# Routing the first rows of a mixture of experts: four gate quadrants at once, running maxima, weight columns in threes

## The chip, the core and the metric

The kernel runs on one core of a Trainium2 chip. The core has TensorE (PE, with its weight loads as PEld), VectorE (DVE), ScalarE (ACT), GpSimd (POOL) and SyncE (SP), each with a queue of its own that it works off in order; DMAs are issued from SP, ACT and POOL. The metric is the device time of one execution in microseconds, the median of several runs.

## The reference

`x` has 64 x 64 tokens of 256 channels, `cond` one row of 64 for each batch entry. There are 8 experts of three layers (256 to 512 to 512 to 256), two of them for each token, all in float32.

```python
var = jnp.mean(x * x, axis=-1, keepdims=True)
xn = rms_w * (x * jax.lax.rsqrt(var + EPS))
gate = xn @ wg_W + wg_b + (genre_embed @ gg_W + gg_b)
gate_w = jax.nn.softmax(gate, axis=-1)
topk_w, topk_i = jax.lax.top_k(gate_w, TOP_K)
cw = jnp.sum(jax.nn.one_hot(topk_i, E, dtype=x.dtype) * topk_w[..., None], axis=-2)
h1 = jax.nn.relu(jnp.einsum('bsh,ehm->bsem', x, W1) + b1)
h2 = jax.nn.relu(jnp.einsum('bsem,emn->bsen', h1, W2) + b2)
out_e = jnp.einsum('bsen,enh->bseh', h2, W3) + b3
return x + jnp.einsum('bseh,bse->bsh', out_e, cw)
```

## The kernel before

Only the two chosen experts of a token are computed. Tokens are sorted by expert into tiles of 128 rows; a tile runs through the three layers of one expert, and its result, scaled by the token's weight for that expert, is added to the output rows by an indirect DMA. The output first receives a copy of `x` (the "fills", DMAs from DRAM to DRAM).

The order of instructions is written out by hand (`manual_schedule`), so each engine's queue stands as the code calls it. The stages are:

- *First part* (`first_part`). Token `p * 32 + i` lies in partition `p`, column `i`. The first 8 columns are part A (1024 tokens), the other 24 part B. Rows are loaded in 8 groups of 4 columns (`load_x` on SP), squared and summed (`squares`, L184 on DVE, L182 on ACT), turned by PE (`turn`, L193; the copies out of PSUM are L204 on DVE and L206 on ACT) and multiplied by the gate weights (`gates`, L211): a matmul writes 32 of the 128 PSUM partitions, a quadrant, and the two halves of the channels are summed there one after the other. `upright` turns the gates back. `Part.root` and `Part.norm` give the inverse root of the mean square; `Part.choose` finds the two highest gates on DVE and writes one-hot rows `oh`; `count` makes running counts `inc` by expert (L312), `totals` sums them over partitions on PE (L324, L325). From part A's counts come slots, a one-hot table `hotA` (L459), and by 16 small matmuls `idxA` (L469), the tokens of the first tile of each expert. `gather` (L680, POOL) then fetches the rows of tile 0 (`xg`), and the weights of the later experts may load.
- *Head steps* `u` = 0 to 6 (`head_step`): layer 1 (L797, relu on ACT L800), turning of the next tile's rows (L733), layer 3 of the tile before (L824), layer 2 (L808, relu L811). In between, `rest` is handed out in pieces (`more`): it routes part B and builds the table of all later tiles (L613, L615, L620 on DVE, L520 on PE), up to `idxR` (L634). `pA.weights` and `pA.spread` (L347 to L350) write the token weights to `cwdA` in DRAM; `gather_cw` fetches the weight columns `cg` of a tile. `scaled` makes `bc` (bias times weight, L784 on ACT), and `give` makes `y` (L833, DVE) and adds it to the output (L834, POOL). The adds wait for each other, and the first one for the fill.
- *Later steps* (from tile 8, the first whose expert is only known at run time): tiles are taken in pairs where they can be, weights are copied on DVE to a fixed place (L758, L763, L767), and rows are turned through DRAM (`stow`, `shuffle`) and DVE (L722). A switch on the number of tiles ends the kernel.

The weights of all experts (`w1a`, `w2a`, `w3a`) are loaded on SP: the three of expert 0 right behind the rows and the biases `vecs` (the source of `vT`, L500), the others after the gather of tile 0. PE's PSUM banks 0, 1, 2 and 5 serve the turned rows, then banks 0 to 3 the layers. POOL makes the identity matrix and clears buffers (L941, L943, L381) before its first DMAs.

Of the kernel before, what the change touches and what calls it, by code (L numbers as in the profile page):

```python
# [21 lines left out]
def kernel(  # L22
# [86 lines left out]
    make_identity(nc, ident)  # L109
    ones = const.tile([P, P], F32, name="ones")  # L110
    nc.gpsimd.memset(ones, 1.0)
# [4 lines left out]
    nc.gpsimd.dma_start(gg_sb[G : G + 1, :], gg_b.unsqueeze(0))  # L116
    nc.gpsimd.dma_start(gg_sb[G + 1 : G + 2, :], wg_b.unsqueeze(0))
    seg = const.tile([P, E, NB], F32, name="seg")
    nc.gpsimd.memset(seg, 1.0)
    nc.gpsimd.memset(seg[:, :, 0:1], 0.0)  # L120
    segA = const.tile([P, E, NA], F32, name="segA")
    nc.gpsimd.memset(segA, 1.0)
    nc.gpsimd.memset(segA[:, :, 0:1], 0.0)
    segT = const.tile([P, NB, E], F32, name="segT")
    nc.gpsimd.memset(segT, 1.0)
    nc.gpsimd.memset(segT[:, :, 0:1], 0.0)
# [81 lines left out]
    def gates(c, bufs, bank=PB[3], q0=0):  # L208

        for q, n in enumerate(bufs, q0):  # L210
            nc.tensor.matmul(  # L211
                bank[32 * q : 32 * q + 32, :],
                lhsT=wg_sb[:, c, :],
                rhs=turned(n),
                start=(c == 0),
                stop=(c == HC - 1),
            )

    def upright(nq, bank=PB[3], dst=PB[4], copied=False):

        R = 32 * nq
        if not copied:
            nc.scalar.copy(gTs[0:R, :], bank[0:R, :])
        gtp = dst[:, 0 : TPB * R].rearrange("p (k r) -> p k r", k=TPB)
        for k in range(TPB):
            nc.tensor.transpose(gtp[:, k], gTs[0:R, ts(k, P)], ident[0:R, 0:R])
        return gtp.rearrange("p k (q e) -> p q k e", q=nq)[:, :, :, 0:E]

    def busy(n):

        for _ in range(n):
            nc.tensor.transpose(PB[6][:, 256 : 256 + P], ident, ident)

    class Part:


        def __init__(self, z, i0, i1):
            self.i0, self.i1, self.n, self.z = i0, i1, i1 - i0, z
            n = self.n
            self.t = {a: t2(f"{a}{z}", n) for a in ("var", "root", "y", "t", "rstd", "m1", "m2", "den", "d2")}  # L240
            self.gate, self.w = t3(f"gate{z}", n), t3(f"w{z}", n)
            self.oh, self.pr = (buf(gx, [P, TOPK, n, E], f"{a}{z}") for a in ("oh", "pr"))
            self.inc = buf(gx, [P, E, n], f"inc{z}")
            self.seg = segA if z == "A" else seg
# [113 lines left out]
    def load_weights(e):  # L358
        w = nc.sync.dma_start(w1a[:, e], W1[e].rearrange("(p c) m -> p c m", c=HC))
        if e:  # L360
            loads.append(w)
# [667 lines left out]
```

## Time and profile before

| | us |
|---|---|
| median of 3 runs | 519.79 (519.06 to 520.1) |
| profiled execution | 521.81 |
| its span | 520.0 |
| PE busy | 499.9 |
| DVE busy | 231.9 |
| ACT busy | 167.9 |
| POOL busy | 291.0 |
| first layer 1 (L797) starts | 25.18 |
| layer 1 of tile 8 starts | 98.59 |

The span runs from the first to the last instruction of the profiled execution; 1.8 us of its time lie around it. A row of a timeline has start, length, engine, line, operation, what is written and read, the sizes and how many instructions; in brackets the idle time before it and what ended that. A float32 matmul has two records. The mean granted TensorE clock was 0.984 of full speed.

### The profile page before, as it was taken

To read this page: it belongs to the slowest core of one execution; us is meant where nothing else is said; L and a number is where in the kernel's file an instruction comes from. 1 tells how busy PE (TensorE), PEld (TensorE's weight loads), DVE (VectorE), ACT (ScalarE), POOL (GpSimd) and SP (SyncE) were. 2 spreads that over 40 slices of the span, in tenths; PEclk is the share of its full clock that TensorE was granted. 3 is DMA by queue.
4 is the path that set the end of the run, shared out by engine and by line. 5 is a ranking of instruction groups with operands and counts; after the bars stand their busy time and mean duration, and the time that the engine had idled before them with its cause. 6 is when DMAs were issued, how large, how long until landed. Compare 5 with 4: busy or idle time off the path is not lost. (4 is left out here: it accounts for less than half of the span.)

```text
span 520.0 us, 8641 instructions
## 1 busy us (share of the span) xinstructions
PE 499.9 (96%) x2834; PEld 447.8 (86%) x2834; DVE 231.9 (45%) x560; ACT 167.9 (32%) x405; POOL 291.0 (56%) x243
## 2 busy tenths in 40 slices
PE   8899979999999999999999999999999999999992
PEld 6579969988888888888888888888888889999991
DVE  5768934343334333344444433433333336555550
ACT  5654324422222222222222222222222223443340
POOL 6314438776655566556566666566566455764521
PEclk9899979999999999999999999999999999999997
DMA  8799993343334343334343333333333333433201
GB/s 333 240 387 404 390 374 109 51 110 77 74 65 89 67 83 69 75 79 83 78 83 74 74 80 75 80 70 80 75 76 75 54 71 53 96 64 74 42 5 22
DMA packets 68160, 59.26 MB, mean 114 GB/s; under 512 B 39663, under 2 KB 59330, under 8 KB 67588
## 3 DMA queue, kind: packets, MB, share of 16 engines
q1 hardware_dynamic: 52464, 41.21, 24.1%
q0 software_dynamic: 15200, 17.32, 20.8%
q8 instruction: 25, 0.41, 0.3%
q14 instruction: 35, 0.29, 0.2%
q10 hardware_dynamic: 436, 0.03, 0.1%
HBM read 42.80 MB, written 20.71 MB: 122 GB/s over the span
## 5 line engine op out<-in xcount | busy, mean ns | idle before, releaser
L808 PE MATMUL pb<-hid,big 128*128 128x256 f32 (+1 forms) x1120 | 210.8, 346 | 0.0
L808 PEld LDWEIGHTS pb<-hid,big 128*128 128x128 f32 x1120 | 187.0, 191 | 20.4
L834 POOL DMA_INDIRECT out_dram<-y,idxR x59 | 97.2, 1648 | 131.3 <-issue 61.4
L811 ACT ACTIVATE hid<-pb,bb 128x256 f32<-128x256 f32 (+1 forms) x140 | 61.5, 440 | 245.7 <-PE pb L808 240.4
L763 DVE COPY big<-w2a 128x2048 f32 x35 | 44.2, 1262 | 162.6 <-PE pb L808 156.8
L797 PE MATMUL pb<-xT,big 128*128 128x256 f32 (+1 forms) x560 | 108.2, 346 | 0.0
L824 PE MATMUL pb<-big,hid 128*128 128x256 f32 x472 | 107.6, 379 | 0.0
L797 PEld LDWEIGHTS pb<-xT,big 128*128 128x128 f32 x560 | 93.5, 191 | 9.9
L824 PEld LDWEIGHTS pb<-big,hid 128*128 128x128 f32 x472 | 88.8, 190 | 11.5
L680 POOL DMA_INDIRECT big<-in_x_dram,idxR x59 | 80.0, 1355 | 20.7 <-issue 16.5
L680 POOL DMA_INDIRECT cg<-cwdR,idxR x59 | 70.1, 1189 | 18.1 <-issue 18.1
L800 ACT ACTIVATE hid<-pb,bb 128x256 f32<-128x256 f32 (+1 forms) x140 | 61.5, 440 | 40.9 <-PE pb L797 26.8
L833 DVE SCALAR_TENSOR_TENSOR y<-pb,cw,bc 128x256 f32<-128x256 f32 x59 | 28.5, 484 | 47.6 <-issue 25.6
L758 DVE COPY big<-w1a 128x1024 f32 x35 | 24.3, 695 | 25.8 <-PE pb L797 22.6
L808 PE MATMUL pb<-hid,w2a 128*128 128x128 f32 x256 | 30.3, 276 | 0.8 <-ACT hid L800 0.8
L808 PEld LDWEIGHTS pb<-hid,w2a 128*128 128x128 f32 x256 | 29.7, 192 | 1.2 <-ACT hid L800 1.0
L767 DVE COPY big<-w3a 128x1024 f32 x35 | 25.5, 729 | 0.5 <-issue 0.5
L834 POOL DMA_INDIRECT out_dram<-y,idxA x8 | 13.5, 1684 | 19.0 <-DVE big L620 6.7
L782 DVE TENSOR_SCALAR bc<-b_sb,cw 128x256 f32 x59 | 22.8, 386 | 2.2 <-DVE cw L779 0.2
L797 PE MATMUL pb<-xT,w1a 128*128 128x128 f32 x128 | 18.0, 297 | 4.8 <-ACT hid L811 3.9
L722 DVE STREAM_TRANSPOSE xT<-gTs 128x256 f32<-128x256 f32 x57 | 22.4, 423 | 0.0
L797 PEld LDWEIGHTS pb<-xT,w1a 128*128 128x128 f32 x128 | 16.7, 209 | 5.3 <-ACT hid L811 4.2
(212 smaller groups left out, 249.2 us busy)
## 6 DMA issues: line engine op xcount, KB each, us to landing
w2a<-in_L_cond_W_dram SPq DMA_DIRECT2D x8, 1024.0 KB
scr<-big SPq DMA_DIRECT2D x57, 128.0 KB
gTs<-scr SPq DMA_DIRECT2D x228, 32.0 KB
w1a<-in_L_cond_W_dram SPq DMA_DIRECT2D x8, 512.0 KB
w3a<-in_L_cond_W_dram SPq DMA_DIRECT2D x8, 512.0 KB
out_dram<-in_x_dram SPq DMA_DIRECT2D x4, 768.0 KB
big<-in_x_dram SPq DMA_DIRECT2D x4, 512.0 KB
big<-in_x_dram SPq DMA_DIRECT2D x2, 1024.0 KB
```

Of the source, the lines that this page charges most:

```text
L680: return nc.gpsimd.indirect_dma_start(out=dst, out_offset=None, in_=src, in_offset=bass.IndirectOffsetOnAxis(ap=index(b), axis=0), bounds_ ...
L758: V.tensor_copy(st1, w1a[:, e].rearrange("p e c m -> p (e c) m"))
L763: V.tensor_copy(st2, w2a[:, ex[u]].rearrange("p e c m -> p (e c) m"))
L767: V.tensor_copy(st3, w3a[:, ex[u]].rearrange("p e c m -> p (e c) m"))
L782: V.tensor_scalar(bc, b3e, cw, None, ALU.mult)
L797: nc.tensor.matmul(ph, lhsT=w1[:, c, ts(m, P)], rhs=cols[:, c, :], start=(c == 0), stop=(c == HC - 1))
L800: nc.scalar.activation(hids[:, 0, m, 0 : w * BT], ph, AF.Relu, bias=bb[:, 0, m : m + 1])
L808: nc.tensor.matmul(ph, lhsT=w2[:, m, ts(n, P)], rhs=hids[:, 0, m, 0 : w * BT], start=(m == 0), stop=(m == MC - 1))
L811: nc.scalar.activation(hids[:, 1, n, 0 : w * BT], ph, AF.Relu, bias=bb[:, 1, n : n + 1])
L824: nc.tensor.matmul(po, lhsT=hids[:, 1, n, ts(k, BT)], rhs=w3[:, n, :], start=(n == 0), stop=(n == MC - 1))
L833: V.scalar_tensor_tensor(y, sums(b), cw, bc, ALU.mult, ALU.add)
L834: add = nc.gpsimd.indirect_dma_start(out=orows, out_offset=bass.IndirectOffsetOnAxis(ap=index(b), axis=0), in_=y, in_offset=None, bounds_c ...
```

## The change

Part A's and the last gates use four quadrants at once, one for each group of rows and half of the channels (`gates_2`); the halves are added when the gates are turned back, by a matmul with `both`, two identity blocks one above the other (`upright_2`). The choice takes a running maximum along each token's 8 gates (a scan that starts anew at each token) in place of a maximum, an equality and a count of equals; one-hot rows are differences of neighbours, and are stored by expert, then column. The count is one scan over both choices; `totals` has three matmuls, one with a negative triangle. Part A takes its square root on ACT as before, part B by integer shift and three Newton steps on DVE. The table of part A is made in four pieces instead of two. All squares of part B and four copies of turned rows are on DVE. Part A's exponentials and `spread` come before the gathers of tiles 1 and 2. Weight columns are gathered three a step in steps 0, 1 and 2 (the last time two), into eight fixed places; `scaled` and `give` start in step 1. Of expert 0 only W1 is loaded ahead of the first gather, `b3` is loaded in two pieces, and most clears move from POOL to DVE, the load of `cond` from ACT to POOL. Longer removed pieces, which stand in the kernel above, are left out here.

```diff
+    nc.gpsimd.dma_start(cond_sb, cond)
+    nc.gpsimd.dma_start(gg_sb[G : G + 1, :], gg_b.unsqueeze(0))
+    nc.gpsimd.dma_start(gg_sb[G + 1 : G + 2, :], wg_b.unsqueeze(0))
     ones = const.tile([P, P], F32, name="ones")
-    nc.gpsimd.memset(ones, 1.0)
+    V.memset(ones, 1.0)
...
+    ntri = const.tile([P, P], F32, name="ntri")
+    V.memset(ntri, -1.0)
+    nc.gpsimd.affine_select(
+        out=ntri, in_=ntri, pattern=[[1, P]], compare_op=ALU.is_ge, fill=0.0, base=0, channel_multiplier=-1
+    )
+    both = const.tile([P, P // 2], F32, name="both")
+    nc.gpsimd.tensor_tensor(both, ident[:, 0 : P // 2], ident[:, P // 2 : P], ALU.add)
+    fresh = const.tile([P, NB, E], F32, name="fresh")
+    V.memset(fresh, 0.0)
+    V.memset(fresh[:, :, 0:1], -BIG)
...
-    def gates(c, bufs, bank=PB[3], q0=0):
-        for q, n in enumerate(bufs, q0):
+    def gates(c, bufs):
+        for q, n in enumerate(bufs):
             nc.tensor.matmul(
-                bank[32 * q : 32 * q + 32, :],
+                PB[3][32 * q : 32 * q + 32, :],
                 lhsT=wg_sb[:, c, :],
                 rhs=turned(n),
-                start=(c == 0),
-                stop=(c == HC - 1),
+                start=c == 0,
+                stop=c == HC - 1,
             )
...
+    def gates_2(bufs, bank):
+        for q, ns in enumerate(bufs):
+            for c, n in enumerate(ns):
+                r = 32 * (2 * c + q)
+                nc.tensor.matmul(bank[r : r + 32, :], lhsT=wg_sb[:, c, :], rhs=turned(n), start=True, stop=True)
+    def upright_2(dst):
+        gtp = dst[:, 0 : TPB * P // 2].rearrange("p (k r) -> p k r", k=TPB)
         for k in range(TPB):
-            nc.tensor.transpose(gtp[:, k], gTs[0:R, ts(k, P)], ident[0:R, 0:R])
-        return gtp.rearrange("p k (q e) -> p q k e", q=nq)[:, :, :, 0:E]
+            nc.tensor.matmul(gtp[:, k], lhsT=gTs[:, ts(k, P)], rhs=both, start=True, stop=True)
+        return gtp.rearrange("p k (q e) -> p q k e", q=2)[:, :, :, 0:E]
...
+            self.oh, self.pr = (buf(gx, [P, TOPK, n * E], f"{a}{z}") for a in ("oh", "pr"))
+            self.ohe = self.oh.rearrange("p k (e i) -> p k e i", e=E)
+            self.pre = self.pr.rearrange("p k (e i) -> p k e i", e=E)
+            self.slot = self.gate.rearrange("p i e -> p (i e)").rearrange("p (e i) -> p e i", e=E)
+            self.inc = buf(gx, [P, 1 + E * n], f"inc{z}")
+            V.memset(self.inc[:, 0:1], 0.0)
             self.cw8 = cw8B[:, i0:i1, :] if z == "B" else t3("cw8A", n)
+            same = gTs[:, 0 : n * (E + 1)] if z == "B" else t2("same", n * (E + 1))
+            self.same = same.rearrange("p (i e) -> p i e", i=n)
+            if z == "A":
+                V.memset(same, 0.0)
...
+        def along(self, t):
+            return t.unsqueeze(2).to_broadcast([P, E, self.n])
+        def norm(self, root):
+            var, y, t = (self.t[a] for a in ("var", "y", "t"))
+            V.tensor_scalar(var, ss[:, self.i0 : self.i1], 1.0 / H, EPS, ALU.mult, ALU.add)
+            if root:
+                nc.scalar.sqrt(t, var)
+                V.reciprocal(y, t)
+            else:
+                V.tensor_scalar(t.bitcast(I32), var.bitcast(I32), 1, None, ALU.arith_shift_right)
+                V.tensor_scalar(y.bitcast(I32), t.bitcast(I32), -1.0, float(0x5F3759DF), ALU.mult, ALU.add)
+            n = 1 if root else 3
+            for k in range(n):
+                V.scalar_tensor_tensor(t, y, -0.5, var, ALU.mult, ALU.mult)
+                V.tensor_tensor(t, t, y, ALU.mult)
+                V.scalar_tensor_tensor(self.t["rstd"] if k == n - 1 else y, t, 1.5, y, ALU.add, ALU.mult)
...
+            gf = gate.rearrange("p i e -> p (i e)")
+            tops = (self.pr[:, 1], self.cw8.rearrange("p i e -> p (i e)"))
+            ms = []
+            for k, (g, top) in enumerate(zip((gf, left), tops)):
+                V.tensor_tensor_scan(
+                    top, fresh[:, 0 : self.n].rearrange("p i e -> p (i e)"), g, 0.0, ALU.add, ALU.max
+                )
+                top = top.rearrange("p (i e) -> p i e", e=E)
+                m = top[:, :, E - 1]
+                ms.append(m)
                 yield
                 if k == 0:
-                    nc.gpsimd.tensor_tensor(self.w, gate, self.over_e(m1), ALU.subtract)
-                V.tensor_tensor(sc, g, self.over_e(m), ALU.is_equal)
+                    nc.gpsimd.tensor_tensor(self.w, gate, self.over_e(m), ALU.subtract)
+                V.tensor_tensor(self.same[:, :, 1:], top, self.over_e(m), ALU.is_equal)
                 yield
...
+                oh = self.ohe[:, k].rearrange("p e i -> p i e")
+                V.tensor_tensor(oh, self.same[:, :, 1:], self.same[:, :, 0:E], ALU.subtract)
                 yield
                 if k == 0:
-                    V.scalar_tensor_tensor(left, sc, -BIG, gate, ALU.mult, ALU.add)
+                    V.scalar_tensor_tensor(
+                        left.rearrange("p (i e) -> p i e", e=E), oh, -BIG, gate, ALU.mult, ALU.add
+                    )
                     yield
...
+            V.tensor_tensor_scan(self.inc[:, 1:], self.oh[:, 0], self.oh[:, 1], 0.0, ALU.add, ALU.add)
+            V.tensor_tensor(self.t["d2"], ms[1], ms[0], ALU.subtract)
...
+            at = self.inc[:, 0 : 1 + E * self.n : self.n]
+            nc.tensor.matmul(self.adj, lhsT=tri, rhs=at[:, 1:], start=True, stop=False)
+            nc.tensor.matmul(self.adj, lhsT=ntri, rhs=at[:, 0:E], start=False, stop=True)
+            nc.tensor.matmul(self.tot, lhsT=ones, rhs=at, start=True, stop=True)
+        def pick(self, dst):
+            V.tensor_tensor(self.pre, self.slot.unsqueeze(1).to_broadcast([P, TOPK, E, self.n]), self.ohe, ALU.mult)
             with nc.allow_low_precision(reason="one term of the sum is not 0, and ranks are exact"):
-                V.tensor_reduce(dst, self.pr, AX.X, ALU.add)
+                V.tensor_reduce(dst, self.pre.rearrange("p k e i -> p k i e"), AX.X, ALU.add)
...
+    def load_weights(e, parts=(0, 1, 2)):
+        for k in parts:
+            dst, src = (
+                (w1a[:, e], W1[e].rearrange("(p c) m -> p c m", c=HC)),
+                (w2a[:, e], W2[e].rearrange("(c p) n -> p c n", p=P)),
+                (w3a[:, e], W3[e].rearrange("(c p) h -> p c h", p=P)),
+            )[k]
+            loads.append(nc.sync.dma_start(dst, src))
+    left = [NA + i for i in (0, 1, 4, 5, 2, 3, 6, 7)] + list(range(NA + 8, NI))
+    def some(n):
+        for _ in range(n):
+            squares(left.pop(0), "V")
...
-        nc.gpsimd.memset(cw8B, 0.0)
+        V.memset(cw8B, 0.0)
+        for k in range(3):
+            V.memset(ring(run, [P, H], "xg", 3, k), 0.0)
+        V.memset(cgR, 0.0)
         nc.gpsimd.dma_start(cwdA.rearrange("(p i) e -> p i e", p=P)[:, NA:NI, :], cw8B[:, NA:NI, :])
-        busy(13)
-        for i, eng in enumerate("VVAA"):
-            squares(i, eng)
+        busy(12)
...
+        squares(TPB + 3, "A")
+        nc.tensor.transpose(cps, cond_sb, ident[:B, :B])
+        V.tensor_copy(condT[0:G], cps.unsqueeze(2).to_broadcast([G, B, REP]))
+        for i in (0, 1):
+            squares(TPB + i, "V")
         for j in range(NG - GA, NG):
             load_x(j)
         nc.sync.dma_start(vecs[0 : E * MC, :], b1.rearrange("e (c p) -> (e c) p", p=P))
         nc.sync.dma_start(vecs[E * MC : 2 * E * MC, :], b2.rearrange("e (c p) -> (e c) p", p=P))
...
+        load_weights(0, (0,))
+        gates_2(((0, 1), (2, 3)), PB[3])
+        pA.norm(True)
+        nc.scalar.copy(gTs, PB[3])
+        turn(GA, 0, 0, "A")
         nc.tensor.matmul(gps, lhsT=condT.rearrange("g b r -> g (b r)"), rhs=gg_sb, start=True, stop=True)
         V.tensor_copy(ggate, gps)
...
+        chosen = pA.choose(upright_2(PB[4]))
+        for q in (1, 2, 3):
...
+        pA.exps()
+        turn_pe(GA + 1, 1, 1)
+        gates(0, range(4))
         for q in range(2):
...
-        GH = GC // 2
+        GH = GC // 4
...
+        load_weights(0, (1, 2))
         tc.add_manual_dep(
-            loads[0].ins,
+            loads[1].ins,
             fetches[0].ins.name,
             mybir.DependencyInfo(mybir.DependencyClass.Sync, mybir.DependencyReason.DATA),
             reason="the first tile's rows go first",
         )
+        load_weights(1, (0,))
+        nc.sync.dma_start(b3_sb[:, 0:2], b3[0:2].unsqueeze(0).to_broadcast([P, 2, H]))
+        load_weights(1, (1, 2))
+        fills.append(nc.sync.dma_start(our[:, 0:NA, :], xr[:, 0:NA, :]))
         load_weights(2)
-        fills.append(nc.sync.dma_start(our[:, 0:NA, :], xr[:, 0:NA, :]))
-        nc.sync.dma_start(b3_sb, b3.unsqueeze(0).to_broadcast([P, E, H]))
+        nc.sync.dma_start(b3_sb[:, 2:E], b3[2:E].unsqueeze(0).to_broadcast([P, E - 2, H]))
...
+    def second_part():
         j0 = GA + 4
+        vps = PB[6][:, 384 : 384 + 2 * E * MC]
+        pA.weights()
+        some(1)
+        nc.tensor.transpose(vps, vecs, ident[: 2 * E * MC, : 2 * E * MC])
+        V.tensor_copy(vT.rearrange("p l e c -> p (l e c)"), vps)
+        some(1)
+        turn(j0, 0, 4, "V")
+        some(2)
+        turn(j0 + 1, 0, 6, "V")
+        gates(1, range(4))
+        some(2)
+        transpose_x(0)
         nc.scalar.copy(gTs, PB[3])
...
+        turn(j0, 1, 5, "V")
+        some(4)
+    def third_part():
+        turn(GA + 5, 1, 7, "V")
+        some(len(left))
+        raw = upright()
         nc.scalar.copy(graw[:, NA : NA + 4 * TPB, :].rearrange("p (q k) e -> p q k e", q=4), raw)
...
+        gates_2(((4, 5), (6, 7)), PB[7])
+        nc.scalar.copy(gTs, PB[7])
+    def last_upright():
+        nc.scalar.copy(
+            graw[:, NA + 4 * TPB : NI, :].rearrange("p (q k) e -> p q k e", q=2), upright_2(PB[6])
...
-        pA.exps()
         V.tensor_scalar(tokv, tokc, 0.0, None, ALU.is_ge)
         V.tensor_tensor(tokv, tokv, tokc, ALU.add)
         V.tensor_copy(tok16, tokv)
-        pB.norm()
...
+        V.memset(pB.same[:, :, 0:1], 0.0)
+        pB.norm(False)
+        yield 2600
...
+    cgR = buf(run, [P, E, E], "cg")
     def gather_cw(u):
         for b in tiles(u):
-            cg = cgs[b] = ring(run, [P, E], "cg", 6, b)
+            cg = cgs[b] = cgR[:, b % E]
             fetch(cg, (cwdA if b < E else cwdR)[:, :], b)
...
-        for k in {0: (), 1: (0, 1), E - 2: (E - 2, E - 1)}.get(u, (u,)):
+        for k in range(3 * u, min(3 * u + 3, E)):
             gather_cw(k)
         n = mms[-1][2] + 1 if mms else 0
         layer1(u)
         if u == 0:
-            last_gates()
+            third_part()
         else:
             more(3200)
         transpose_x(u + 1)
         stage_1(u + 1)
-        if u >= 3:
+        if u >= 1:
             scaled(u - 1, "A")
-        if u >= 1:
             layer3(u - 1)
         table(n)
         n = mms[-1][2] + 1 if mms else 0
         if u:
             more(3200)
-        layer2(u, None if u else pB.root)
+        layer2(u, None if u else last_upright)
         table(n)
         if u <= 1:
             more(1 if u else 3200)
...
+        if u >= 1:
             give(u - 1)
...
-        some, left = first_part()
-        for b in range(3):
+        first_part()
+        gather(0)
+        other_loads()
+        second_part()
+        pA.spread(cwdA, pA.cw8, 0)
+        for b in range(1, 3):
             gather(b)
-        other_loads()
-        second_part(some, left)
         other = rest()
```

## The prediction

> **What bounds the kernel now.** I read the page's busy line and clock slices, then the windows, then the timeline of each engine up to 100 us.
>
> ```profile
> PE 499.9 (96%) x2834; PEld 447.8 (86%) x2834; DVE 231.9 (45%) x560; ACT 167.9 (32%) x405; POOL 291.0 (56%) x243
> ...
> PEclk9899979999999999999999999999999999999997
> ...
> 200.00:300.00 100.00, 100.00 (x465) 88.03 (x465) 38.76 (x86) 27.00 (x57) 59.94 (x43) 1.00 0.39 77
> ```
>
> The windows' columns are stretch, sum, then PE, PEld, DVE, ACT, POOL busy, clock, DMA. From about 95 us to 500 us PE never stops and the clock is whole, and the change leaves the later tiles' instructions as they are. So only the head can gain, and its gain is how much earlier the first later tile (step 8, layer 1 at L797) starts; it starts at 98.59 us. Where does PE lose time before that? First in step 5:
>
> ```profile
> 52.30 1.64 POOL L834 DMA_INDIRECT out_dram<-y,idxA  x1 [2.79 <-DVE y L833]
> 60.63 1.56 POOL L834 DMA_INDIRECT out_dram<-y,idxA  x1 [6.70 <-DVE big L620]
> 62.50 1.07 POOL L680 DMA_INDIRECT xg<-in_x_dram,idxA  x1 [0.30 <-PE pb L824]
> 63.88 1.72 POOL L680 DMA_INDIRECT cg<-cwdA,idxA  x1 [0.30 <-issue]
> 70.63 0.51 ACT L784 ACTIVATE bc<-b_sb,cg 128x256 f32<-128x256 f32 x1 [9.44 <-DMA cg<-cwdA,idxA]
> 71.44 3.79 PE L797 MATMUL pb<-xT,w1a 128*128 128x128 f32 x16 [3.43 <-ACT hid L811]
> ```
>
> POOL's second add to the output stands until 60.63, though its y was ready at 52.4 (L833 ends); DVE is named, but the first add must have landed, and the third's wait does name the add's DMA. The weight column (cg) of tile 3 is queued behind it, is issued at 63.88 and lands at 70.63. ACT waits for it in order, the relus of layer 2 stand behind, and PE stops for 3.43 us. Then it runs slowly: the row has 3.79 us for what took 2.03 at 58.43 us, and windows of half a microsecond show the clock at 0.50 from 70.2 to 77.0. Start to start, the four groups from 71.44 to 78.93 took 7.49 us against 4.80 from 58.43 to 63.23: 2.69 us more. PE waits 0.51 at 50.90 and 0.83 at 87.77 too, behind gaps of ACT that nothing in the trace explains. Losses after the count of part B: 3.43 + 2.69 + 0.51 + 0.83 = 7.46 us.
>
> The second view is DVE, against the PE row that waits for the count of part B:
>
> ```profile
> 28.29 0.08 DVE L184 DVE_READ_ACCUMULATOR2_ANT ss<- 128x1 f32 x1
> ...
> 33.04 0.30 DVE L261 RECIPROCAL yB<-rootB 128x24 f32<-128x24 f32 x1 [3.77 <-ACT rootB L256]
> ...
> 40.85 0.56 DVE L312 TENSOR_TENSOR_SCAN incB<-seg,prB 128x192 f32<-128x192 f32 x1
> ...
> 41.46 0.39 PE L324 MATMUL pb<-incB,tri 128*128 128x8 f32 x2
> ```
>
> The count ends at 41.41 and PE comes to it at 41.46: the two are even. DVE had 3.77 us of slack waiting for ACT's square root, and 1.67 before L500. Whatever makes PE earlier from here is lost unless DVE is earlier too.
>
> **The change part by part.**
>
> *Front, up to the first rows.* Two gate rows:
>
> ```profile
> 7.79 2.03 PE L211 MATMUL pb<-hid,wg_sb 128*32 128x512 f32 x8 [0.68 <-DVE ss L184]
> 13.57 1.06 PE L211 MATMUL pb<-hid,wg_sb 128*32 128x512 f32 x8
> ```
>
> The first writes two quadrants twice, the second four quadrants once. Part A's gates become of the second kind: -0.97. The copy of the gates then stands on ACT behind the root of var, which DVE ends at about 8.7, so only about 0.5 of it comes through to the first product (10.98). From there to the count's end (15.03) were 14 DVE operations and 4.05 us; now 10, scans at 0.32 and the rest at 0.26 to 0.31 with their hand-over: 2.9, -1.15. A third total matmul: +0.2. The one-hot table in four pieces leaves 4 matmuls behind the last piece instead of 8: -0.3. So idxA ends at 17.6 to 18.0 instead of 19.27; I take 17.8.
>
> The Trainium skill, "SBUF — State Buffer" (SBUF: two separate sides), calls the ports shared by VectorE and GpSimd an exclusive lock. The two L391 operations, 8 columns wide, took 1.27 and 1.40 us while POOL cleared buffers (6.4 to 7.7), and other 8-wide operations 0.17. By the rule, moving those clears to DVE frees about 1 us, idxA at 17.3; by the rows ACT's copy (to 7.74) let the gates start no earlier than 7.79. I give it nothing beyond the 0.5. The 13 clears on DVE, 0.1 to 0.3 us each, end before the rows land at 4.38, which is their cover. cond's load moves from ACT's queue to POOL's, ahead of the identity's second half: PE's idle transposes start up to 0.8 later, under the same cover.
>
> First rows: gather 17.8 to 18.9, landed at 20.7 (before: issued by 20.67, W1 of expert 1 released at 22.52, 1.85 later). On POOL part A's weights (0.32 + 0.48 + 0.41, DMA 0.62: rows L347 to L350) now go ahead of gathers 1 and 2: gather 1 is issued by 22.2 instead of 21.99, lands under load by 27, and is wanted at about 26.5. Of the loads only W1 of expert 0 stands ahead, but DMA was already at 0.18 in 20 to 22.5, so leaving W2 and W3 behind saves nothing here. It puts 1.5 MB (3.7 us at 405 GB/s) after the gather. From 22.5 to 27.5 before, DMA moved 1.33 MB; so W2 of expert 0, 1 MB from 20.8, is there at about 25.6 to 27. Layer 2 wants it at 27.5. Either may be 2 us late under the wait below. On SP b3's pieces, the fill and later weights slip similarly by at most 2 us, and PE wants W1 of expert 2 at 42 against about 40.
>
> Layer 1 of step 0 starts at about 23 instead of 25.18, with a 0.7 us wait inside for a DVE copy of bank 1 that ACT made before.
>
> *DVE after idxA.* In queue order: part A's weights 0.65; 24 squares at the pitch of 0.467 (L184), where 16 stood: 11.2; vT 0.2; 4 copies of turned rows, formerly ACT's, at 0.62 (L204): 2.5; constants 0.6; part B's root by 12 operations at 0.22 (L262 to L265): 2.6; then choice and count. On choice a page speaks against the change: "SBUF — State Buffer" (Door 1: The DMA port swizzle and its notes) says SBUF lines are 16 bytes and each crossing is paid, free only to 4 fp32 of stride. The choices are now laid out by expert, 24 elements apart for B. The trace:
>
> ```profile
> L311 DVE TENSOR_TENSOR prA<-ohA x1: 273/273/273, 14.4 to 14.4; 128x64 f32<-128x64 f32 x1
> L311 DVE TENSOR_TENSOR prB<-ohB x1: 629/629/629, 40.2 to 40.2; 128x192 f32<-128x192 f32 x1
> ```
>
> So the step of 24 costs 0.63 for 0.36, the step of 8 only 0.27 for 0.22, though the page would charge both: by the page part A's three strided steps cost 0.36 more and idxA is at 18.2. I take the rows: product, sum, scan, equal, difference, left, scan, equal, difference, count = 0.39 + 0.39 + 0.58 + 0.39 + 0.64 + 0.64 + 0.58 + 0.39 + 0.64 + 0.58 = 5.2. Sum 22.95, with about 0.8 waiting for PE's turns and vecs (1.67 before): 17.8 + 22.95 + 0.8 = 41.55, and up to 1 more where the clock is at half speed around 20 us, as it was (0.51 in 20 to 22.5): I take **42.0** against 41.41. The square root on DVE saves no table load (two loads before and after); it removes the wait on ACT, whose slack the squares and copies now fill.
>
> *PE up to the count.* Step 0 gets gates of 1.06 for 1.91 and no 0.73 wait, but a set of turns and four upright transposes, about 1.0, and the 0.7 above; with step 1 it comes to the count at about 39.6. So PE waits about 2.4 us for DVE, a new wait, with layer 1 of step 2 and all later steps queued behind the totals; the 2 us of the front are gone there.
>
> *From the count to step 8.* Before 98.59 - 41.46 = 57.13, less 7.46 of losses = 49.67; a third total matmul +0.2. The weight columns are fetched in threes in steps 0 and 1, before any add: cwdA, written at about 21, landed after 5.5 before (39.08 to 44.59), hence 26.6; columns 0 to 2 issued by 30.5, 3 to 5 by 36, landing 5 us later. Column 3, wanted by ACT at about 58, is 18 us early. Extra issue on POOL delays gather 4 only, to about 31, wanted at 52. The adds stay in line (1.9 + 6.3 us each), gathers 5 to 7 behind them at about 48, 56, 64, wanted from 60, 69, 78. The output scaling moves one step up: bc on ACT 0.4 between relus, y on DVE 0.48; two y's stood ahead of the table already. DVE from count to first table piece: 52.33 - 41.41 = 10.9, less waits of 1.46, plus 0.4 (PE), 0.4 (two subtractions), 0.3 for the strided reduce: 52.5, ready at 56.6; PE comes at 42.05 + 15.5 + 0.2 = 57.7. So it holds. I leave 0.5 for ACT gaps such as the two unexplained ones (0 to 1.34).
>
> Step 8 then starts at 42.05 + 49.87 + 0.5 = 92.4: **-6.2 us**. The profiled execution took 521.81 (span 520.0), 2.0 over the median: it would be 515.6, the median 519.79 - 6.2 = **513.6**.
>
> **The rivals.**
> 1. *Cold clock after the new wait.* "TensorE: Matmul & The Clock Gate" (Why this matters for your kernels) puts the fall at idle gaps over about 3 us; by it 2.4 us is harmless. Against it, the clock also fell at 19.0, after only 0.87 us of idle amid transposes and 8-column matmuls. Price: a window of 3.4 us at half speed, 1.7, or two, 3.4: 515.3 to 517.0. 25%.
> 2. *DVE is quicker than summed* (the waits for PE vanish, the count ends by 40.5) and no ACT gaps: 519.79 - 8.2 = 511.6. 13%.
> 3. *Slower: ACT stands in step 1 for column 0.* bc moved from step 2 to step 1; ACT takes it at about 35, and layer 2's relus and so PE queue behind. I have column 0 at 32.6. The wait at the count covers another 2.4; to lose everything it must land 2.4 + 2.4 + 6.2 us later, past 43.6. Against: POOL's gathers beside DVE's squares took 1.0 to 1.1 us. For: in threes behind cwdA, which took 5.5 us under load. At 46: 522. 8%.
> 4. *No change*: DVE's table or late weights eat the 6 us again: 519.8. 4%.
>
> **How the numbers follow.** The first case has 50%, its own range 512.6 to 514.8. Adding rivals 1 and 2 with their bounds: 511.0 to 517.5. Within 0.2% (1.0 us, about what can be measured here) lies rival 4. Faster 0.88, same 0.04, slower 0.08.
>
> **What would show it.** idxA at 17.8; layer 1 of step 0 at 23; a PE wait of about 2.4 us before the first total of part B, count at 42; no ACT wait for cg, no stall in step 5; step 8 at 92.4. Wrong if PE waits for a DMA, if the count is past 44, or if the clock shows 0.5 after 40 us.

## The result and the profile after

The changed kernel takes 516.57 us (median of 7 runs, 515.05 to 517.18) beside 519.23 us for the kernel before (7 runs, 518.83 to 521.47): a ratio of 0.9934, 95% interval 0.9915 to 0.9953. It is faster, by 2.7 us by the medians and 3.4 us by the ratio, where 6.2 us had been forecast. The profiled execution took 516.57 us with a span of 514.7, so it sits on its own median, while the profiled execution of before (521.81) is 2.6 us above its median of these runs. The two traces are therefore 5.3 us apart and the medians only about 3.

The page first, its busy line, the clock of its 40 slices and one stretch of the windows (columns: stretch, sum, then PE, weight loads, DVE, ACT, POOL, clock, DMA share, GB/s):

```profile
PE 498.2 (97%) x2845; PEld 446.4 (87%) x2845; DVE 238.6 (46%) x589; ACT 165.2 (32%) x390; POOL 292.9 (57%) x229
PEclk9799999999999999999999999999999999999997
200.00:300.00 100.00, 100.00 (x465) 88.04 (x464) 38.52 (x85) 27.63 (x59) 61.65 (x45) 1.00 0.39 77
```

From 200 to 300 us the row is as it was before (PE 100.00, clock 1.00); what changed is in the head. The timelines of PE (layer 1 of steps 2, 5 and 8), ACT and POOL:

```profile
44.16 0.39 PE L343 MATMUL pb<-incB,tri 128*128 128x8 f32 x2 [1.56 <-DVE incB L337]
44.85 2.03 PE L817 MATMUL pb<-xT,w1a 128*128 128x128 f32 x16
...
69.95 2.03 PE L817 MATMUL pb<-xT,w1a 128*128 128x128 f32 x16
...
93.28 3.62 PE L817 MATMUL pb<-xT,big 128*128 128x256 f32 x16
```
```profile
37.80 0.51 ACT L804 ACTIVATE bc<-b_sb,cg 128x256 f32<-128x256 f32 x1
...
63.18 0.52 ACT L804 ACTIVATE bc<-b_sb,cg 128x256 f32<-128x256 f32 x1
```
```profile
27.24 1.00 POOL L698 DMA_INDIRECT cg<-cwdA,idxA  x1 [0.30 <-issue]
...
32.76 1.09 POOL L698 DMA_INDIRECT cg<-cwdA,idxA  x1 [0.30 <-issue]
...
47.94 1.64 POOL L854 DMA_INDIRECT out_dram<-y,idxA  x1 [7.21 <-DVE offs L580]
...
56.31 2.00 POOL L854 DMA_INDIRECT out_dram<-y,idxA  x1 [2.47 <-DVE big L631]
58.62 1.25 POOL L698 DMA_INDIRECT xg<-in_x_dram,idxA  x1 [0.31 <-issue]
```

The stall of 3.43 us in step 5 is gone. The column that made it, that of tile 3, is fetched at 32.76 (63.88 before), ahead of all adds, and ACT takes it at 63.18 without a wait. Column 0 is fetched at 27.24 (44.59 before) and taken at 37.80, also without a wait; the first add is at 47.94 (52.30 before); step 5 runs its 16 matmuls in 2.03 us, as at whole clock. Step 8 starts at 93.28 instead of 98.59. But step 2 starts at 44.85 where it had started at 41.93: the head up to the count of part B became nearly 3 us slower, and PE now waits 1.56 us there for DVE. The front, up to the first rows:

```profile
2.60 2.82 PE L245 MATMUL pb<-ident 128*128 128x128 f32 x12 [2.60 <-POOL ident masks.py:199]
5.36 0.26 PE L416 MATMUL pb<-ident,gTs 2*128 2x2 f32 x1
...
7.93 1.83 PE L226 MATMUL pb<-hid,wg_sb 128*32 128x512 f32 x8
...
10.79 1.08 PE L232 MATMUL pb<-both,gTs 128*128 128x64 f32 x8 [0.32 <-ACT gTs L441]
```
```profile
5.85 1.04 DVE L419 TENSOR_SCALAR wg_sb<-wg_in,rwT 128x8 f32<-128x8 f32 x2
...
11.90 0.23 DVE L303 TENSOR_TENSOR gateA<-pb,rstdA 128x64 f32<-128x64 f32 x1 [0.82 <-PE pb L232]
...
19.09 0.17 DVE L481 SCALAR_TENSOR_TENSOR idxA<-pb,sa 128x8 int32<-128x8 f32 x1
```

The first product of the gates (L303) comes at 11.90 instead of 10.98, and idxA ends at 19.26 as before (19.27). From 16.5 to 23.3 us, 6.8 us or twice 3.4, PE ran at half clock (windows of the trace after):

```profile
12.00:16.50 4.50, 3.25 (x29) 2.62 (x31) 3.49 (x15) 3.20 (x6) 0.33 (x1) 1.00 0.60 229
16.50:23.30 6.80, 6.80 (x45) 4.51 (x41) 4.72 (x20) 2.25 (x4) 3.05 (x6) 0.50 0.07 22
```

### The profile page after: what moved, and what is told of

Its sections match the earlier page's. It is cut to its first block, busy times and chain, and to the rows that moved or that the text cites. A ratio compares the mean times of both kernels' runs of the same rounds, so it can differ in the third digit from the quotient of the medians.

```text
span 514.7 us, 8676 instructions
## 1 busy us (share of the span) xinstructions
PE 498.2 (97%) x2845; PEld 446.4 (87%) x2845; DVE 238.6 (46%) x589; ACT 165.2 (32%) x390; POOL 292.9 (57%) x229
## 5 line engine op out<-in xcount | busy, mean ns | idle before, releaser
L698 POOL DMA_INDIRECT big<-in_x_dram,idxR x59 | 81.0, 1373 | 21.3 <-issue 16.5
L698 POOL DMA_INDIRECT cg<-cwdR,idxR x59 | 69.0, 1169 | 18.0 <-issue 17.7
L831 ACT ACTIVATE hid<-pb,vT 128x128 f32<-128x128 f32 x32 | 11.8, 368 | 26.2 <-PE pb L828 26.2
L817 PE MATMUL pb<-xT,w1a 128*128 128x128 f32 x128 | 16.2, 278 | 0.4 <-DVE big L206 0.4
```

The source lines that it names most:

```text
L698: return nc.gpsimd.indirect_dma_start(out=dst, out_offset=None, in_=src, in_offset=bass.IndirectOffsetOnAxis(ap=index(b), axis=0), bounds_ ...
L817: nc.tensor.matmul(ph, lhsT=w1[:, c, ts(m, P)], rhs=cols[:, c, :], start=(c == 0), stop=(c == HC - 1))
L831: nc.scalar.activation(hids[:, 1, n, 0 : w * BT], ph, AF.Relu, bias=bb[:, 1, n : n + 1])
```

## The experiments

All ratios are to runs of the kernel before on the same chip (519.23 us beside the changed kernel, 519.86 to 520.15 beside the others, so ratios compare better than medians). w0 stands for all three weights of expert 0.

| kernel | median us | ratio to before | 95% interval |
|---|---|---|---|
| changed | 516.57 | 0.9934 | 0.9915 to 0.9953 |
| before + columns early (e1) | 520.19 | 1.0000 | 0.9988 to 1.0012 |
| changed, columns and adds late (e2) | 522.20 | 1.0043 | 1.0033 to 1.0054 |
| changed, adds late (a1) | 518.55 | 0.9968 | 0.9955 to 0.9982 |
| before + columns, adds, root (f1) | 514.42 | 0.9893 | 0.9862 to 0.9924 |
| f1 with ACT's root (f2) | 515.25 | 0.9903 | 0.9870 to 0.9936 |
| changed, front mended (e3) | 516.19 | 0.9926 | 0.9902 to 0.9950 |
| changed, copies on ACT (e4) | 515.93 | 0.9911 | 0.9890 to 0.9931 |
| e4 + rows of tile 1 first (g1) | 514.65 | 0.9893 | 0.9862 to 0.9925 |
| g1 + w0 ahead (h1) | 514.52 | 0.9899 | 0.9867 to 0.9931 |
| changed + w0 ahead (h2) | 517.33 | 0.9930 | 0.9903 to 0.9957 |
| h1 + front (h3) | 513.67 | 0.9862 | 0.9833 to 0.9891 |

**The columns alone, on the kernel before.**

```
-            cg = cgs[b] = ring(run, [P, E], "cg", 6, b)
+            cg = cgs[b] = ring(run, [P, E], "cg", 8, b)
...
-        for k in {0: (), 1: (0, 1), E - 2: (E - 2, E - 1)}.get(u, (u,)):
+        for k in {1: (0, 1, 2), 2: (3, 4, 5), 3: (6, 7)}.get(u, ()):
```

> The kernel before, with one edit: weight columns 0 to 2 are fetched in step 1, 3 to 5 in step 2, 6 and 7 in step 3 (eight places instead of six), so columns 2 to 5 no longer stand behind an add; routing, gates, loads and the place of the output scaling are as before. Theory (the gain of the change is the removed wait for the weight columns): the 3.43 us stall in step 5 and the half clock behind it go, step 8 starts 3.4 to 6 us earlier, at 92.6 to 95.2, and the time is 513.2 to 515.8 if the kernel before takes 519.2. Rival (the gain comes from the new gates and choice): within 0.6 us of the kernel before.

The ratio is 1.0000: the theory in this form fell, and by its time alone the rival would have stood. The trace says otherwise (its execution, 522.55 us, is the longest of the 14). Timelines of POOL and PE of this kernel:

```profile
64.66 2.46 POOL L834 DMA_INDIRECT out_dram<-y,idxA  x1 [5.92 <-DVE y L833]
67.42 2.00 POOL L680 DMA_INDIRECT xg<-in_x_dram,idxA  x1 [0.30 <-PE pb L808]
...
69.54 2.03 PE L797 MATMUL pb<-xT,w1a 128*128 128x128 f32 x16
76.09 0.70 PE L733 MATMUL pb<-ident,xg 128*128 128x128 f32 x2 [4.52 <-DMA xg<-in_x_dram,idxA]
```

Layer 1 of step 5 has no stall at 69.54, and then PE waits 4.52 us for the rows of tile 6. The three fetches ahead of the first add pushed it to 55.60 and the second to 64.66; the rows that stand behind the second add come late instead of a column. So the bound of this stretch is the line of adds on POOL, and what stands behind the second one pays. One limit: this kernel still writes the weights to `cwdA` where the kernel before does, so its first column is issued only at 45.59 and the columns stand in the adds' way. The changed kernel writes them at 22 us.

**The same part taken out of the changed kernel**, whole (columns one a step, scaling and adds a step later) and by half (only scaling and adds later). The edit of the half; the whole also has the old line of column fetches:

```
+        if u >= 3:
+            scaled(u - 1, "A")
         if u >= 1:
-            scaled(u - 1, "A")
             layer3(u - 1)
...
-        if u >= 1:
+        if u == 2:
+            scaled(0, "A")
+            scaled(1, "A")
+            give(0)
+        if u >= 2:
             give(u - 1)
```

> The changed kernel with the weight columns fetched one a step, and the output scaling and adds at the steps where the kernel before has them; gates, choice, root and loads stay as changed. Theory (the columns are the gain): a stall of 3 us or more for a column in step 4 or 5 comes back and the time is 519 or more, as long as the kernel before. Rival (gates and choice are the gain): within 0.6 us of the changed kernel, 516 to 517.

> The changed kernel with its weight columns three a step, but the output scaling (bc) and the adds one step later, where the kernel before has them. Theory (after the two column experiments: what is lost behind the second add is the gain, whichever transfer stands there, and the change avoids it by columns ahead of the adds and by adds one step earlier, both needed): the first add at about 52.5 instead of 47.94, the second 8 us later at 60.5 to 61, the rows of tile 6 behind it at 62.5 to 64.5, landed at 70 to 71.5 and wanted at 69; PE waits 1 to 2.5 us there, and the time is 518 to 520. Rival (columns ahead of the adds are enough): no wait for rows of tile 6, 516 to 517 as the changed kernel.

With both late the time is 522.20, and the stall is back (timelines of ACT and PE):

```profile
74.91 0.51 ACT L804 ACTIVATE bc<-b_sb,cg 128x256 f32<-128x256 f32 x1 [8.98 <-DMA cg<-cwdA,idxA]
...
75.72 2.77 PE L817 MATMUL pb<-xT,w1a 128*128 128x128 f32 x16 [2.96 <-ACT hid L831]
```

With the adds alone late it is 518.55. The time was as the theory had it and the place was not: the first add is at 55.41, the second at 63.36, the rows of tile 6 are issued at 65.21, and PE waits for no rows in steps 5 and 6; the loss is spread over small gaps (0.83 and 0.41 us in step 1, about 0.4 us in step 6), whose cause the trace does not show. By the ratios the columns, once they are early, bring 1.0043 - 0.9968 = 0.75% (3.9 us) and the adds' place 0.9968 - 0.9934 = 0.34% (1.8 us; the intervals end just apart, at 0.9955 and 0.9953). It is not only a matter of the clock: at a granted clock of 0.992 or more the median is 517.1 us (6 executions) for late adds and 515.5 (3) for the changed kernel, at 0.990 or less 518.8 (16) and 516.6 (3).

**That part alone on the kernel before**, with what it needs: part A's weights computed and written early, behind the gathers of tiles 0 to 2, part B's root on DVE, the fill and two rows of b3 earlier. Two of its edits:

```
+        pA.weights()
+        pA.spread(cwdA, pA.cw8, 0)
...
-        for k in {0: (), 1: (0, 1), E - 2: (E - 2, E - 1)}.get(u, (u,)):
+        for k in range(3 * u, min(3 * u + 3, E)):
```

> The kernel before with these parts of the change alone: part A's exponentials, weights and their write right behind its indices, the root of part B on VectorE (so that ACT needs no third table), weight columns three a step from step 0, output scaling and adds one step earlier, and the two bias rows and the fill that these need loaded earlier. Gates in two quadrants, the old choice, and all of expert 0's weights ahead stay. Theory (columns and adds are the whole gain; gates, choice and loads bring nothing): no PE wait in steps 4 to 6, step 8 at 92 to 94, time 513.5 to 516.6, as fast as the changed kernel or faster. Rival (the new gates and choice are needed for it): 517.5 to 519.5.

> The kernel with the columns and adds alone, but with the root of part B by ScalarE's table as in the kernel before, between the exponentials of part A and of part B: two more table loads of 1.28 us on ScalarE. Theory (one root table is what lets the columns come early without a stall): ScalarE's loads stand between relus of layer 2 in step 0, PE waits 1 to 1.5 us there, and the time is 0.7 to 1.7 us longer, 515.1 to 516.1. Rival (ScalarE has the room): 514 to 514.9, as with the root on VectorE.

514.42 us: faster than the changed kernel by the medians. The list of PE's waits has none in steps 2 to 6, and step 8 starts at 90.74. So this part is enough for the whole gain. What this kernel leaves out of the change (gates in four quadrants, running maxima, squares and copies moved to DVE, W1 alone ahead, part A's weights ahead of the gathers of tiles 1 and 2) together shows no gain; by the ratios it costs 0.4%, about 2 us, though the two intervals overlap. With ACT's root the kernel is 0.5 us longer by the ratios (0.83 by the medians), and two table loads of 1.28 us appear; the first holds ACT between relus. PE's layer 2 of step 0 took 3.74 us with either root, so the wait that was expected there did not come. The intervals overlap, so no loss is shown. Timelines of DVE and ACT, of the kernel with DVE's root and then with ACT's:

```profile
36.55 0.56 DVE L323 TENSOR_TENSOR_SCAN incB<-seg,prB 128x192 f32<-128x192 f32 x1
...
42.36 0.16 DVE L557 TENSOR_TENSOR mm<-more,pb 128x8 f32<-128x8 f32 x1 [5.19 <-PE pb L336]
```
```profile
33.02 1.28 ACT L256 ACT_TABLE_LOAD   x1
34.31 0.22 ACT L256 ACTIVATE rootB<-varB 128x24 f32<-128x24 f32 x1
34.44 0.61 ACT L821 ACTIVATE hid<-pb,vT 128x128 f32<-128x128 f32 x2
```

DVE's count ends at 37.11 and DVE then waits 5.19 us for PE: with 16 squares and no copies DVE is far from the bound, even with the old choice (13 operations from the gates to the count) and the longer root. PE came to the count at 41.14 (41.46 before), so 4.3 us on DVE alone brought 0.3.

**What makes the rest slow.** First the front, then DVE:

```
-    nc.gpsimd.dma_start(cond_sb, cond)
...
-    nc.gpsimd.iota(iotx, [[1, P], [0, GC]], base=0, channel_multiplier=0, allow_small_or_imprecise_dtypes=True)
...
+    nc.gpsimd.iota(ior, [[1, P]], base=0, channel_multiplier=0, allow_small_or_imprecise_dtypes=True)
...
+        nc.scalar.dma_start(cond_sb, cond)
...
+        V.tensor_copy(iotx, ior.unsqueeze(2).to_broadcast([P, P, GC]))
```

> The changed kernel with its first 7 us mended: the load of cond is back on ACT's queue, the two small bias loads stand behind POOL's other work, and POOL writes a row of 128 indices that DVE spreads to 128x2048 while it is idle (3 to 5.5 us) instead of a 2.5 us iota on POOL beside DVE's first operations. Theory (the front lost 1 us to the late identity and to POOL's iota): PE's idle transposes start at 1.6 instead of 2.6, L419's two operations take 0.2 to 0.4 each instead of 0.9 to 1.0, the first product of the gates is at 10.9 to 11.2 instead of 11.90 and idxA at 18.2 to 18.6 instead of 19.26; of that 0.3 to 1.0 us reach the end, since DVE's count of part B bounds step 2. Rival (rows land when they land and PE's clock sets the front): idxA within 0.3 of 19.26, and the time unchanged.

```
-        turn(j0, 0, 4, "V")
+        turn(j0, 0, 4, "A")
```

(and the same for copies 5, 6 and 7)

> The changed kernel with the four copies of turned rows 4 to 7 on ACT instead of DVE. Theory (DVE's extra work makes the count of part B late): DVE loses 4 x 0.62 = 2.5 us before the count, which ends at 41.6 to 42.2 instead of 44.11; PE comes to it at about 42.6, so its wait of 1.56 us goes and the time falls by 1.2 to 1.6 us, to 515.0 to 515.4 if the changed kernel takes 516.6. Rival (PE or ACT sets this stretch, DVE only fills it): the copies delay ACT's relus of step 0, and the time is unchanged or up to 1 us longer.

The mended front (timelines of DVE and PE):

```profile
5.11 0.37 DVE L421 TENSOR_SCALAR wg_sb<-wg_in,rwT 128x8 f32<-128x8 f32 x2
...
8.51 0.22 PE L432 MATMUL pb<-ident,cond_sb 64*64 64x64 f32 x1 [0.54 <-DMA cond_sb<-in_cond_dram]
8.65 1.06 PE L224 MATMUL pb<-hid,wg_sb 128*32 128x512 f32 x8
```

The two 8-wide operations take 0.37 us together instead of 1.04 and end 1.4 us earlier (5.48, 6.89 in the changed kernel), but cond, on ACT's queue, now lands after PE comes to it: PE stands for it ahead of the gates, DVE's copy and squares behind it wait too, and idxA ends at 19.33. The time came free and went into another wait, as the rival had it. The clock happened to stay whole from 16 to 23 us, though PE was as idle before it as in the changed kernel, and fell after PE's wait of 1.56 us for the count. Windows of that kernel, and the row of that wait:

```profile
12.00:16.50 4.50, 3.25 (x31) 2.82 (x33) 3.42 (x14) 3.20 (x6) 0.34 (x1) 1.00 0.63 215
16.50:23.30 6.80, 6.21 (x55) 3.92 (x47) 5.81 (x24) 2.35 (x5) 2.98 (x6) 1.00 0.08 25
...
44.80:48.30 3.50, 3.50 (x16) 3.23 (x16) 3.26 (x20) 2.11 (x6) 1.33 (x1) 0.51 1.01 408
```
```profile
43.18 0.39 PE L341 MATMUL pb<-incB,tri 128*128 128x8 f32 x2 [1.56 <-DVE incB L335]
```

With the copies on ACT the count came at 42.76 (44.11 in the changed kernel) and PE's wait for it was gone, but PE waited 2.09 us for the rows of tile 1 instead:

```profile
30.49 0.48 PE L753 MATMUL pb<-ident,xg 128*128 128x128 f32 x2 [2.09 <-DMA xg<-in_x_dram,idxA]
```

Step 2 started at 44.82 against 44.85: in the trace the gain was taken back by the next wait, and the intervals of the two times overlap. The change puts part A's weights ahead of that gather on POOL. So it was moved:

```
         gather(0)
+        gather(1)
         other_loads()
         second_part()
         pA.spread(cwdA, pA.cw8, 0)
-        for b in range(1, 3):
-            gather(b)
+        gather(2)
```

> The changed kernel with the four copies of turned rows 4 to 7 on ACT, and the gather of tile 1 on POOL ahead of part A's weights instead of behind them. Theory (with the copies on ACT the count was early but tile 1's rows, issued at 23.4 and landed at 30.5, became the bound): tile 1's gather is issued at 20.9 and landed by 28, PE's 2.1 us wait and the half clock behind it at 32 to 35.8 go, step 1 starts at 34 to 34.5 instead of 36.9, the count ends by 42, and step 2 starts at 42.2 to 43 instead of 44.8; 513.5 to 514.8. Rival (the weight loads then come late instead): a new wait for w2 or w3 of expert 0, and 515.5 to 516.5.

514.65 us, 1.9 us less than the changed kernel by the medians (the intervals overlap a little), as fast as columns and adds alone, which also have that gather first. The wait for tile 1 is gone and step 2 starts at 43.67, later than expected; PE stands 0.82 and 0.94 us in step 1 for nothing that the profile names. Late weights were the suspect:

```
-        load_weights(0, (0,))
+        load_weights(0)
...
-        load_weights(0, (1, 2))
+        load_weights(1, (0,))
...
```

> As the one with tile 1's rows first, and besides all three weights of expert 0 loaded ahead of the first rows, as in the kernel before. Theory (leaving w2 and w3 of expert 0 behind the rows leaves the DMA engines idle from 12 to 17 us and puts every later weight 1.5 MB, 3.7 us, later; with the other waits gone PE meets it in step 1, as waits of 0.82 and 0.94 us): those two waits go, step 1 takes 8 us instead of 10.4, step 8 starts at 90 to 91 instead of 92.1, and the time is 512.6 to 513.6. Rival (the waits are ACT's or an artefact of the records): 514.2 to 515.

> The changed kernel with all three weights of expert 0 ahead of the first rows, and nothing else. Theory (late weights are hidden in the changed kernel itself, behind VectorE's late count): within 0.7 us of the changed kernel, 516 to 517. Rival (late weights and rows of tile 1 under their load are what makes it slow): 514 to 515.5.

Neither moved (514.52 and 517.33, ratios 0.9899 against 0.9893 and 0.9930 against 0.9934): the order of expert 0's weights makes no difference that these runs show, though from 16.5 to 23.3 us DMA has a share of 0.10 without them (g1) and 0.65 with them (h1). A gap of 1.11 us in step 1 was there again with the weights ahead. Such a gap ends just as a late relu of ACT ends (35.61 and 35.56 us in g1, 37.29 and 37.24 in h1; ACT idle for 2.23 and 1.78 us before it); why ACT stands there is open.

The last kernel fills PE's wait for the choice with nine idle transposes. Tried alone on the kernel with tile 1's rows first (g2), they wrote into the bank from which part A's gates are read. L303 waited for them until 14.79 and read what they had left, so that kernel routes by false gates, and its 537.10 us (ratio 1.0340) say nothing of the fill. What the fill alone is worth was not measured.

> As the one with tile 1's rows first and all of expert 0's weights ahead, with the front mended further: cond by SyncE's queue, identity ahead of all loads on POOL, the index table spread by DVE from a row of 128, part A's gates in two quadrants with four transposes of 64 rows instead of products with the folded identity, and nine idle transposes on PE during the choice. Theory: first product at 11 to 11.3 instead of 11.90, idxA at 18.2 to 18.7 instead of 19.26, clock whole from 16 us on, layer 1 of step 0 at 22.7 to 23.3, and 0.5 to 1 us less than the kernel without it: 511.8 to 513. Rival (rows of tile 0 land no earlier, or DVE's count sets step 2): the same as without it.

513.67 us, ratio 0.9862, the best of all, though short of the expected 511.8 to 513; its parts were run together, so each is read from the trace (timelines of PE and DVE, and windows):

```profile
8.14 2.10 PE L450 MATMUL pb<-hid,wg_sb 128*32 128x512 f32 x8
...
10.91 0.46 PE L237 MATMUL pb<-ident,gTs 64*128 64x64 f32 x4
...
22.91 0.71 PE L828 MATMUL pb<-xT,w1a 128*128 128x128 f32 x4
```
```profile
11.41 0.23 DVE L308 TENSOR_TENSOR gateA<-pb,rstdA 128x64 f32<-128x64 f32 x1 [0.24 <-PE pb L237]
...
18.52 0.17 DVE L493 SCALAR_TENSOR_TENSOR idxA<-pb,sa 128x8 int32<-128x8 f32 x1
```
```profile
12.00:16.50 4.50, 4.41 (x39) 3.52 (x39) 3.47 (x14) 3.29 (x6) 0.34 (x1) 1.00 0.99 361
16.50:23.30 6.80, 6.17 (x54) 4.33 (x51) 5.94 (x28) 4.14 (x9) 3.63 (x6) 1.00 0.66 216
```

The four transposes take 0.46 us where the folding products took 1.08, idxA ends at 18.69, the clock is whole, and layer 1 of step 0 starts 2.07 us earlier than in the changed kernel (22.91 against 24.98). The clock was whole there without the fill too, in the traces of e2, e3, e4, g1 and h2 (step 0 at 23.81 in g1), so it is not shown that the fill did it. Of the 2.07 us, 0.85 is left in the time against the kernel without it (h1); among executions with a granted clock of 0.992 or more, five of each, 0.56 us.

## Why the prediction was right or wrong

**The direction and the place were right, the size was not.** The gain is the removed wait in step 5. From the count to step 8 it took 49.12 us (44.16 to 93.28), forecast 49.87 and 0.5 for gaps. Rival 3 did not come: columns landed 5.6 to 6.9 us after issue, so column 0 was there by about 34, and ACT took it at 37.80. The measured 516.57 us lies outside the favoured case (512.6 to 514.8) and inside the whole range only through the share of rival 1, whose cold clock after the new wait the trace does not have (1.00 from 40 to 48.3 us). That the range held is luck.

**The reason was incomplete.** The prediction gave the fetches in threes all of it and listed the adds' move as a cost of ACT and DVE work. On the kernel before, where their weights are written late, fetches in threes bring nothing (e1), since the rows of tile 6 take the column's place behind the second add; in the changed kernel they bring 3.9 us and the adds' place another 1.8 (a1). It also said that the root on DVE "saves no table load" against the kernel before. That is so (two loads each), but with part A's exponentials early it saves two (f2 against f1); a gain in time from that is not shown.

**idxA at 17.8 was wrong by 1.46.** The term that failed is the first product of the gates: 0.5 us was to come through from faster gates, and it came 0.92 later. The prediction has ACT's copy of the gates stand behind the root of var, "which DVE ends at about 8.7". DVE ended var at 9.92. Timelines of DVE before, then of DVE, ACT and POOL after:

```profile
4.38 0.43 DVE L184 CUSTOM_DVE_ANT_0 sqV<-big 128x256 f16<-128x256 f32 x1 [3.15 <-DMA big<-in_x_dram]
...
8.39 0.20 DVE L255 TENSOR_SCALAR varA<-ss 128x8 f32<-128x8 f32 x1
```
```profile
5.66 0.16 DVE L417 COPY rwT<-pb 128x2 f32<-128x2 f32 x1 [2.51 <-PE pb L416]
...
9.75 0.17 DVE L283 TENSOR_SCALAR varA<-ss 128x8 f32<-128x8 f32 x1
```
```profile
9.96 0.21 ACT L285 ACTIVATE tA<-varA 128x8 f32<-128x8 f32 x1 [1.09 <-DVE varA L283]
10.08 0.57 ACT L441 COPY gTs<-pb 128x512 f32<-128x512 f32 x1
```
```profile
4.38 2.47 POOL L130 IOTA iotx<- 128x2048 f16 x1
```

Before, two of DVE's four squares of part A stood in its queue behind nothing but two clears, and ran as the rows landed. Now all four stand behind L417, which waits 2.51 us for PE's L416, and that stands behind twelve idle transposes, which the late identity starts at 2.60 instead of 1.53. From 5.66 on DVE works without a gap up to var. The section on the change does not name this move, the sum has no term for it, and no run took it back alone. The prediction gave the identity's delay as covered by rows landing at 4.38; L416 at 5.36 shows that it was not.

The gates ended at 9.76, hardly ahead of var: the four-quadrant row took 1.06 where its inputs were all there (e3), and 1.83 here, where they came one by one. The folded products, left out of the sum, took 1.08 for transposes of 0.46. The clears moved to DVE freed little: L419 still took 1.04 us (1.41 before), beside POOL's iota, and ended with it (6.89 and 6.85). The lock that the Trainium skill, "SBUF — State Buffer" (SBUF: two separate sides), describes fits the rows: 1.04 us beside the iota, 0.37 without it in e3. What the iota cost idxA was not measured apart: in e3 cond's wait stood in its place, and in h3, with neither, var ended at 9.61 but gates in two quadrants held ACT's copy until 10.28.

Of the rest, the choice was right (2.91 us from 11.90 to 14.81, forecast 2.9), while from the count's end to idxA 4.45 us passed where 0.1 less than 4.24 was forecast (4.32 in e3, at whole clock): gates at half clock stood before the table's matmuls.

**Layer 1 of step 0 at 23 was wrong by 2.** PE came to it at half clock, which lasted to 23.3. With the clock whole and idxA no earlier (19.33), e3 started it at 23.53; with idxA 0.57 earlier as well, h3 started it at 22.91.

**The count at 42.0 was 44.11**, past the 44 that the prediction itself had named as a sign of being wrong. The sum had given 41.55, and 0.45 was added for the half clock. From 41.55 to 44.11 are 2.56 us: 1.46 of them is idxA; DVE then waited 0.76 + 0.49 + 0.42 = 1.67 us for PE where 0.8 was given (PE at half clock), 0.87 more; and the first difference with 24-element steps took 0.86 beside POOL's subtraction (40.01 to 40.72), the second 0.62 without it, 0.24 more. The price of 0.63 for the strided operation held. PE's new wait was there, 1.56 for 2.4, since PE was late too. The two differences on DVE:

```profile
40.35 0.86 DVE L329 TENSOR_TENSOR ohB<-gTs 128x192 f32<-128x192 f32 x1
...
42.89 0.62 DVE L329 TENSOR_TENSOR ohB<-gTs 128x192 f32<-128x192 f32 x1
```

**The size.** Between the traces the forecast was 98.59 to 92.4, measured 93.28: 0.9 us off, by a count 2.1 later and a way from there 1.25 quicker. The larger error is the base: 2.69 us of clock loss was taken from one execution, and the result was set against the median, which that execution exceeds by 2.6. Which of its losses the median execution lacks is not settled, as only profiled executions show their rows. Rival 1 (cold clock after the new wait) did not come in the profiled execution of this kernel, but half clock followed the same wait of 1.56 us in e3 (0.51 from 44.8 us) and one of 1.88 us in e2 (0.55 from 45.8 us). The Trainium skill, "TensorE: Matmul & The Clock Gate" (Why this matters for your kernels), by which a gap has to pass about 3 us, does not hold for these rows. The 22 executions of a1 give an idea of how often clock is lost, though not where: six have a mean granted clock of at least 0.994, five of them at 516.74 to 517.26 us and one at 518.16; the other sixteen, at 0.987 to 0.990, took 518.08 to 519.94 us.

## What to carry to other kernels

When a transfer waits behind others in one queue, ask what stands behind it before pricing its removal: here the rows took over the wait from the column, and only columns fetched ahead of every add, with the adds earlier too, brought the whole gain. A stretch in which two engines arrive together gains little from either alone (DVE's count came 4.3 us earlier in f1, PE's 0.3); work moved to the engine that then arrives last comes back as a wait (1.56 us of PE for DVE's count). When the order of a queue changes, follow what stood first in it: here two squares that had run while rows landed now stand behind a wait, and var came 1.3 us later. Take losses of clock from several executions, not from the one that was profiled.

## What the runs showed of the hardware

Beside a 128x2048 iota on POOL, which reads nothing, two 8-wide DVE operations took 1.04 us together, and 0.37 and 0.43 us in the two kernels where the iota is 128x128 and over by then (e3, h3).

The half clock comes in stretches of about 3.4 us or twice that (16.5 to 23.3 us in the changed kernel, 44.8 to 48.3 in e3). One and the same idle pattern of PE, 3.25 to 3.27 us busy of the 4.5 from 12.0 to 16.5, was followed by it in the traces of three kernels (0.50 to 0.53 from 16.5 to 23.3 us: the changed kernel, a1 and h1) and not in five others (1.00 in e2, e3, e4, g1 and h2). So a wait of 1.2 to 2.1 us is priced by itself and, in some executions, by another 1.7 us for each 3.4 us stretch. With the wait filled by nine transposes (4.41 busy of 4.5) the clock stayed whole in the one trace taken, which is too few to show that the fill helps.
